# A Mamba layer and a linear attention on one core: the ration of TensorE's work by even and odd slots, and the slot of the convolution's first products

## The chip, the cores and the metric

The kernel runs on one core of one Trainium2 chip. The metric is the device time of one execution in microseconds. Three runs of the kernel before took 8108.69, 8114.99 and 8093.1 us; the median is 8108.69 us.

The engines are named as the profile names them: PE is TensorE (PEld its weight loads), DVE is VectorE, ACT is ScalarE, POOL is GpSimd, SP is SyncE, whose queue issues most DMAs.

## The reference, cut to what matters

The input x is 4 images of 512 channels and 64 x 64 positions. Two layers follow each other, each on a group-normed input and added to it.

```python
x = x + mamba_layer(_gn(x))       # layer 0
x = x + linear_attention(_gn(x))  # layer 1
```

Layer 0 takes the 4096 positions of an image as a sequence, norms each position over its channels, and cuts the channels into 4 groups of 128. Each group is a sequence of its own for the same Mamba block:

```python
xi, z = split(x @ in_proj_w.T)                   # 256 channels each
xc = silu(conv1d(xi, 4 taps) + conv_b)
dt, Bs, Cs = split(xc @ x_proj_w.T)              # rank 8, 16 states, 16 states
dt = softplus(dt @ dt_proj_w.T + dt_proj_b)
h = exp(dt * A) * h + (dt * xc) * Bs             # a scan over the positions, per channel and state
y = (sum over states of h * Cs + xc * D_param) * silu(z)
y = y @ out_proj_w.T
```

A skip is added, the result is normed again over the channels and projected. Layer 1 forms q, k (with relu) and v, sums k times q over all positions of an image, and only then can apply that sum to v and project. So an image's attention begins when its last Mamba tile is through.

## The kernel before, in words

**Steps and slots.** The work is cut into 128 steps: image b, tile t of 512 positions, channel group c (the innermost). A step is done in 16 slots (`SLOTS`), one for each half e of the 256 inner channels, each of four groups q of states and each half jj of the blocks of channels. The loop thus has 2048 slots. Slot s of a step in the text is the slot with that number, 0 to 15.

**What a slot issues** (`slot`, from line 618, and the functions that it calls). On POOL `drive(g + 2)` makes the input bx of the slot two ahead (L614, 128x1024). On DVE there are two scans (L632, 128x512); behind each of them ACT makes the decay dA of a scan three ahead (L606). After the first scan comes `product(g - 1)` (L655): the states of the slot before are multiplied by c_all, which TensorE has spread over the partitions into a PSUM bank of its own (`c_row`, one bank, one c_all for two slots). The exception is in `BEHIND`, the slots 4 and 11: their product comes at the end of the slot itself, so that a wide DVE operation which stands at the end of slot 3 or 10 (`AWAY`) has its place. After the product of an odd slot, TensorE is given the next c_all, and then `fold_states`, which sums the states into y. The last quarter of the positions is multiplied on POOL instead (L643).

So DVE's order around slot 4 is: two scans of slot 3, a wide operation or none, scan, product(3), scan, product(4), two scans of slot 5 and so on. TensorE's c_all for the slots 4 and 5 can only start after product(3), since it overwrites the bank that product(3) reads, and product(4) is the first to need it. The c_all for slots 6 and 7 starts after product(5) and is first needed by product(6), in slot 7.

**What else a slot carries** is issued by `after()`, at the end of each slot, by the slot's number:
- slots 0 and 1: the last parts of `mixers` of the step after the next; the spread of d_all in slot 1
- slot 2: `time_banks`, two banks pt for the step width dt; slot 3: `time_steps`, two softplus on ACT that read them (L512), between two loads of ACT's table
- slots 3, 5, 6, 7, 8 and 9: one part each of `inputs` (`front`) of the step after the next. The first part is two taps of the convolution for one half (pc, two products of 128x512), the second the other two taps; the third and fourth do the same for the other half; the last two are pz
- slot 4: `to_rows`, on POOL (L520) and as DMAs on SP, and `out_proj` (po, three products' worth)
- slot 6: the copy of po back (L690), and, as due one slot after the second part of `inputs`, the copy of pc (L484)
- slots 10 and 12 to 15: silu, and the parts of `mixers`

**Three queues of pieces** fill in the rest: `ahead` (the norm of the next tile), `late` (the norm and projection of the tile just done) and `rest` (the attention of an image that is done, which runs beside the next image's Mamba). Each slot takes at most one piece of each. Whether it may depends on `credit`: each slot adds its ration, takes away the products that were issued since (`work["mm"]`, in which a 128x512 fp32 product counts 1, bf16 a quarter, and four abreast count a quarter each), and what is saved up is limited. A piece of `late` or `rest` is issued while the credit is above zero. The pieces' wide DVE operations (L386, L406) go to slots 3 and 10.

**Banks.** The products of `inputs`, of `time_banks`, `out_proj`, `mixers` and of all pieces share three PSUM banks (`ps_w`), handed out in turn: whoever takes a bank waits until the engine that reads its last content is done. TensorE works in the order of issue, so what is behind a waiting product waits too.

Of the kernel before, what the change touches and what calls it, by code (L numbers as in the profile page):

```python
# [24 lines left out]
def kernel(  # L25
# [100 lines left out]
    work = {"mm": 0.0}  # L126
# [376 lines left out]
    def time_banks(f, nm):  # L503

        f["pt"] = [work_bank(f"pt_{nm}_{e}", 0) for e in range(NH)]
        for e in range(NH):
            r = slice(e * LANE, (e + 1) * LANE)
            mm(f["pt"][e], w_dt[r, :], f["dtr"][r, :], start=True, stop=True, abreast=NH)
# [16 lines left out]
    def spread(f, e, nm):  # L525

        d = wk.tile([P, 2, NJ, T], F32, tag="d_all", name=f"d_all_{nm}_{e}")
        for v in range(2):
            src = f["d_rows", v].rearrange("(j i) e t -> i e j t", i=BLK)[:, e]
            for k in range(KS):  # L530
                nc.sync.dma_start(d[k * BLK : (k + 1) * BLK, v], src)  # L531
        f["d_all", e] = d

    def mixers(f, nm):

        pd = work_bank(f"pd_{nm}", 0)
        for e in range(NH):
            mm(pd, w_xp[:, e, :], f["xz"][:, 0, e, :], start=(e == 0), stop=(e == NH - 1))  # L540
        yield
        f["both"] = wk.tile([P, 2, NH, T], F32, tag="dt", name=f"dt_{nm}", bufs=1)
        dtr = f["dtr"] = f["both"][0 : 2 * LANE, 1, NH - 1, :]
        nc.scalar.copy(dtr, pd[0 : 2 * LANE, :])
        b_rows = f["b_rows"] = dram.tile([NST, T], F32, tag="b_rows", name=f"b_rows_{nm}", bufs=3)
        c_rows = f["c_rows"] = dram.tile(
            [NST, T - CUT], F32, tag="c_rows", name=f"c_rows_{nm}", bufs=3
        )

        def rows_out():  # L550
            nc.sync.dma_start(b_rows, dtr[RANK : RANK + NST, :])
            nc.sync.dma_start(c_rows, dtr[LANE : LANE + NST, CUT:])

        later(1, rows_out)
        parts = f["parts"] = wk.tile([P, CUT], BF16, tag="parts", name=f"parts_{nm}", bufs=3)
        nc.scalar.copy(parts, pd[:, :CUT])
        for i in (2, 3):
            yield
            mm(pd[:, :CUT], minus, parts, start=False, stop=True, skip_group_check=True)
            yield  # L560
            nc.scalar.copy(parts[i * LANE :, :], pd[i * LANE :, :CUT])
# [113 lines left out]
    def take_y(f, n, e):  # L675
        nc.scalar.copy(f["xz"][:, 0, e, :], ys.pop((n, e)))  # L676

    def gate(f, e):
        nc.gpsimd.tensor_tensor(  # L679
            f["xz"][:, 1, e, :], f["xz"][:, 1, e, :], f["xz"][:, 0, e, :], ALU.mult  # L680
        )
# [234 lines left out]
    def input_norm(b):  # L916
        stats = stats_tile(f"st0_{b}")
        yield from stats0(stats, b)
        norms[b] = yield from stats_end(stats, f"a{b}")
        yield  # L920

    def tile_norm(b, t):
        xn[b, t] = wk.tile([P, NC, NTAP - 1 + T], F32, tag="xn", name=f"xn_{b}_{t}", bufs=3)
        pads[b, t] = small.tile([P, NC, NTAP - 1], F32, tag="pad", name=f"pad_{b}_{t}")
        yield from normed(
            xn[b, t], pads[b, t], pads[b, t - 1] if t else None, b, t, norms[b]
        )
# [13 lines left out]
    def step_inputs(n):  # L941
        b, t, c = steps[n]
        return inputs(fs[n], xn[b, t], c, names[n])
# [6 lines left out]
    def add_to(queue, pieces):  # L950
        queue.append([pieces, None])
# [40 lines left out]
    with tc.manual_schedule():  # L992
        credit, seen, mix, held[0], held_x[0] = 0.0, work["mm"], iter(()), 0, 0
        for n, (b, t, c) in enumerate(steps):
            f, nm = fs[n], names[n]
            before = fs[n - 1] if n else None
            nxt = fs[n + 1] if n + 1 < N else None
            front = step_inputs(n + 2) if n + 2 < N else iter(())
            last_mix, mix = mix, mixers(fs[n + 2], names[n + 2]) if n + 2 < N else iter(())
            if c == 0 and (t + 1 < NT or b + 1 < B):  # L1000
                add_to(ahead, tile_norm(b, t + 1) if t + 1 < NT else tile_norm(b + 1, 0))
            if c == 0 and t == 0 and b + 1 < B:
                add_to(light, input_norm(b + 1))
            assert c != 2 or not ahead
            for s in range(SLOTS):
                def after():
                    nonlocal credit, seen
                    now[0] = n * SLOTS + s
                    for what in [w for at, w in due if at <= now[0]]:
                        what()  # L1010
                    due[:] = [d for d in due if d[0] > now[0]]
                    if s == 0 and before is not None:
                        take_y(before, n - 1, 1)
                    if s == SLOTS // 2:
                        take_y(f, n, 0)
                    if s < 2:
                        next(last_mix, None)
                    if s == 1:
                        spread(f, 1, nm)
                        if before is not None:  # L1020
                            gate(before, 1)
                    if s == 2 and nxt is not None:
                        time_banks(nxt, names[n + 1])
                    if s == 3 and nxt is not None:
                        nc.scalar.preload_act_table_set("softplus")
                        time_steps(nxt, names[n + 1])
                        nc.scalar.preload_act_table_set("natural_log_exp_and_others")
                    if s == 6 and before is not None:
                        pb_, pt_, pc_ = steps[n - 1]
                        with_skip(before, xn[pb_, pt_], pc_)  # L1030
                        if pc_ == NC - 1:
                            add_to(late, leave(pb_, pt_))
                    if s in (3, 5, 6, 7, 8, 9):
                        next(front, None)
                    if s == 4 and nxt is not None:
                        to_rows(nxt, 0, names[n + 1])
                        to_rows(nxt, 1, names[n + 1])
                    if s == 4 and before is not None:
                        pb_, pt_, pc_ = steps[n - 1]
                        out_proj(before, xn[pb_, pt_], pc_, names[n - 1])  # L1040
                    if s == 9:
                        gate(f, 0)
                        if nxt is not None:
                            spread(nxt, 0, names[n + 1])
                    if s == 10 and n + 2 < N:
                        silu(n + 2)
                        nc.scalar.preload_act_table_set("natural_log_exp_and_others")
                    if s >= 12:
                        next(mix, None)
                    may = [  # L1050
                        what for k, what in ((0, "wide"), (1, "one ahead"), (2, "two ahead"))
                        if any(a - 2 * k <= s <= a - k for a in AWAY) or (k == 2 and s == SLOTS - 1)
                    ]
                    if light and light[0][1] == "wait" or s in AWAY and not any(
                        q and q[0][1] == "wide" for q in (ahead, late)
                    ):
                        one(light)

                    limit[0] = 1 if 0 < s < 6 else 2
                    credit = min(credit + 3.5 - (work["mm"] - seen), 2.6)  # L1060
                    busy = False
                    for queue in (ahead, late, rest):
                        kind = queue[0][1] if queue else None
                        if queue is ahead or kind == "free" or credit > 0 or kind == "more" and not busy:
                            start = work["mm"]
                            one(queue, ANYWHERE if queue is ahead and (c, s) > (1, 4) else may)
                            credit -= work["mm"] - start
                            busy = busy or work["mm"] - start > 1
                    seen = work["mm"]

                slot(n * SLOTS + s, N * SLOTS, after)
            fs[n - 1].clear() if n else None
        product(N * SLOTS - 1, N * SLOTS)
        now[0] = None
        for _, what in due:
            what()
# [60 lines left out]
```

## Time and profile before

| | before |
|---|---|
| median of 3 runs | 8108.69 us |
| profiled execution: time | 8103.21 us |
| profiled execution: span | 8101.5 us |
| loop, first scan to last product | 118.7 to 7631.7 us |
| DVE busy | 7158.1 us (88% of the span) |
| POOL busy | 6888.6 us (85%) |
| PE busy | 6487.2 us (80%) |
| ACT busy | 5365.5 us (66%) |
| mean granted clock of PE | 0.887 |

A group line of the profile reads: line, engine, operation, tiles written and read (buffer numbers left out), shapes, count | busy us, mean ns of one | idle time of the engine just before them, and what ended most of it. In a timeline, the first number is the start in us from the start of the span, the second the time taken, and brackets hold the idle time before it with what ended it. The granted clock is the share of TensorE's full speed that its throttle let through.

### The profile page before, as it was taken

The page shows a single profiled execution, that of the slowest core. Times are in us where ns is not written, and L with a number is a line of the kernel's source. Part 1 is how long each engine was busy: PE and PEld are TensorE (multiplying, and loading weights), DVE is VectorE, ACT ScalarE, POOL GpSimd, SP SyncE. Part 2 cuts the span into 40 slices and gives each one's busy share as a digit, 9 for nine tenths or more (in the row PEclk, how much of TensorE's full clock was granted, in tenths as well). Part 3 has the DMA queues.
Part 4 walks back from the last instruction along what each step waited for, and adds up shares of the span by engine and source line. Part 5 has one row for each costly group of instructions (what it writes and reads, how often), then busy time and mean ns, then how long its engine had stood idle before and what let it go on. Part 6 is the DMA issues. An engine that isn't in the chain of part 4 may idle for free.

```text
span 8101.5 us, 92105 instructions
## 1 busy us (share of the span) xinstructions
PE 6487.2 (80%) x24800; PEld 2116.5 (26%) x24800; DVE 7158.1 (88%) x6891; ACT 5365.5 (66%) x7841; POOL 6888.6 (85%) x4597
## 2 busy tenths in 40 slices
PE   5677777667888888887788888888788888888699
PEld 1111112111222222322132222222122222322144
DVE  5999999999999999999999999999999999999700
ACT  4666677676677767676777767676777777766421
POOL 4999999999999988899989989898999989889600
PEclk8787878788899999998898999899799999999699
DMA  5666666666666666676756666677666666677402
GB/s 159 167 164 159 154 147 153 157 155 166 162 169 156 156 161 153 173 191 169 170 144 171 165 163 159 149 182 184 157 163 157 154 154 148 157 185 187 113 32 88
DMA packets 829195, 1265.95 MB, mean 156 GB/s; under 512 B 183912, under 2 KB 317560, under 8 KB 816384
## 3 DMA queue, kind: packets, MB, share of 16 engines
q1 hardware_dynamic: 804736, 1222.32, 60.1%
q0 software_dynamic: 16896, 33.56, 2.4%
q10 hardware_dynamic: 7040, 4.20, 0.2%
q8 instruction: 194, 3.18, 0.2%
q14 instruction: 329, 2.70, 0.1%
HBM read 1052.78 MB, written 206.57 MB: 155 GB/s over the span
## 4 chain that ended last, share of the span: by engine, by line
DVE 21%; PE 19%; DMA 19%; POOL 15%; issue 10%; SPq 9%; ACT 6%; POOLq 0%; DVEq 0%; ACTq 0%
DVE h L632 13%; POOL bx L614 11%; DMA d_all<-d_rows 11%; DVE h L655 6%; SPq L581 6%; PE pq L124 5%; DMA b_all<-b_rows 4%; SPq L531 3%; ACT dA L606 3%; PE pc L124 3%; PE pr L124 3%; PE y L124 2%; DMA c_sb<-c_rows 2%; POOL h L643 2%; POOL dt L520 1%
## 5 line engine op out<-in xcount | busy, mean ns | idle before, releaser
L614 POOL TENSOR_TENSOR bx<-d_all,b_all 128x1024 f32<-128x1024 f32 x2048 | 4815.8, 2370 | 51.4 <-DVE h L632 34.1
L632 DVE TENSOR_TENSOR_SCAN h<-dA,st,bx 128x512 f32<-128x512 f32 x3584 | 4425.2, 1268 | 59.0 <-ACT dA L606 49.5
L606 ACT ACTIVATE dA<-d_all,a_t 128x512 f32<-128x512 f32 x4096 | 2787.8, 689 | 1936.0 <-DVE h L632 1893.6
L655 DVE TENSOR_TENSOR h<-h,c_all 128x768 f32<-128x768 f32 x2048 | 1908.8, 932 | 301.9 <-PE c_all L124 293.5
L643 POOL TENSOR_TENSOR h<-h,c_sb 128x512 f32<-128x512 f32 x1024 | 1298.6, 1268 | 145.8 <-DMA c_sb<-c_rows 49.7
L124 PE MATMUL y<-h,fold 128*32 128x512 f32 x8192 | 1287.8, 705 | 140.7 <-POOL h L643 136.9
L124 PE MATMUL c_all<-parts,sel 128*128 128x384 bf16 x1024 | 369.8, 361 | 1112.7 <-DVE h L655 1110.5
L124 PE MATMUL pc<-xn,w_cv 128*128 128x512 f32 x2048 | 1068.2, 657 | 189.4 <-DVE xn L406 127.2
L124 PE MATMUL pq<-w_qk,xa 128*128 128x512 f32 x2048 | 989.8, 616 | 1.6 <-ACT xa L344 1.6
L632 DVE TENSOR_TENSOR_SCAN h<-dA,bx 128x512 f32<-128x512 f32 x512 | 601.6, 1207 | 60.3 <-ACT dA L606 55.9
L124 PEld LDWEIGHTS pc<-xn,w_cv 128*128 128x128 f32 x2048 | 394.1, 203 | 819.3 <-issue 455.9
L124 PEld LDWEIGHTS <-sel 128*128 128x128 bf16 x1280 | 127.5, 100 | 1792.5 <-DVE h L655 1552.8
L642 POOL COPY st<-h 128x4 f32<-128x4 f32 x1024 | 207.3, 202 | 436.4 <-DVE h L632 392.9
L124 PEld LDWEIGHTS pq<-w_qk,xa 128*128 128x128 f32 x2048 | 404.2, 200 | 455.6 <-issue 432.3
L124 PE MATMUL pr<-xb,m 128*128 128x512 f32 x1024 | 503.8, 630 | 7.3 <-DMA xb<-x 4.0
L124 PE MATMUL pp<-xn,w_pr 128*128 128x512 f32 x1024 | 487.5, 602 | 3.8 <-DVE xn L406 3.8
L124 PEld LDWEIGHTS y<-h,fold 128*32 128x32 f32 x8192 | 171.0, 115 | 719.2 <-issue 291.0
L124 PE MATMUL y<-xz,dg 32*32 32x512 f32 x2048 | 340.5, 741 | 0.0
L679 POOL TENSOR_TENSOR xz<-xz 128x512 f32<-128x512 f32 x256 | 325.0, 1270 | 2.7 <-ACT xz L676 2.7
L124 PE MATMUL pd<-xz,w_xp 128*128 128x512 f32 x512 | 317.3, 752 | 7.8 <-ACT xz L946 7.8
L520 POOL TENSOR_TENSOR dt<-dt,xz 128x1024 f32<-128x1024 f32 x128 | 302.1, 2360 | 22.1 <-DMA c_rows<-dt 20.9
L730 ACT ACTIVATE kq<-pq 128x512 f32<-128x512 f32 x256 | 150.9, 590 | 242.9 <-PE pq L124 240.0
(156 smaller groups left out, 5919.5 us busy)
## 6 DMA issues: line engine op xcount, KB each, us to landing
d_all<-d_rows SPq DMA_DIRECT2D x2048, 256.0 KB, 6.6
b_all<-b_rows SPq DMA_DIRECT2D x4096, 64.0 KB, 2.2
d_rows<-dt SPq DMA_DIRECT2D x256, 512.0 KB, 3.7
c_sb<-c_rows SPq DMA_DIRECT2D x4096, 16.0 KB, 1.8
xs<-in_x_dram SPq DMA_DIRECT2D x32, 1024.0 KB, 6.5
xn<-in_x_dram SPq DMA_DIRECT2D x32, 1024.0 KB, 5.8
xr<-in_x_dram POOLq DMA_DIRECT2D x32, 1024.0 KB, 10.6
x<-xr SPq DMA_DIRECT2D x32, 1024.0 KB, 6.6
```

The costliest lines, as they stand in the source:

```text
L124: nc.tensor.matmul(out_, lhsT, rhs, **how)
L520: nc.gpsimd.tensor_tensor(f["both"][:, 1], f["both"][:, 0], f["xz"][:, 0], ALU.mult)
L531: nc.sync.dma_start(d[k * BLK : (k + 1) * BLK, v], src)
L581: nc.sync.dma_start(dst[k * BLK : (k + 1) * BLK, :], rows_[q * KS + k, :].partition_broadcast(BLK))
L606: nc.scalar.activation(dAs[k], fs[n]["d_all", e][:, 0, j, :], AF.Exp, scale=a_t[:, e, j, q : q + 1])
L614: nc.gpsimd.tensor_tensor(bxs[g], fs[n]["d_all", e][:, 1, jj * 2 : jj * 2 + 2, :], bc(b_all[g // JJ], 2), ALU.mult)
L632: nc.vector.tensor_tensor_scan(h[:, j, :], dAs.pop(2 * g + i), bxs[g][:, i, :], 0.0 if t == 0 else st[:, c, e, q, j : j + 1], ALU.mult, AL ...
L642: nc.gpsimd.tensor_copy(st[:, c, e, q, :], h[:, :, T - 1])
L643: nc.gpsimd.tensor_tensor(h[:, :, CUT:], h[:, :, CUT:], bc(c_sb.pop(g // JJ), NJ), ALU.mult)
L655: nc.vector.tensor_tensor(own, own, bc(c_all[g // JJ], 2), ALU.mult)
L679: nc.gpsimd.tensor_tensor(f["xz"][:, 1, e, :], f["xz"][:, 1, e, :], f["xz"][:, 0, e, :], ALU.mult)
L730: nc.scalar.activation(qk[i], pq, AF.Relu)
```

## The change

The first part of `inputs`, the two taps that open the convolution's first bank, is issued in slot 4 instead of slot 3. In slot 4 it stands ahead of `out_proj`, as the code has it.

The ration, 3.5 in every slot with at most 2.6 saved up, becomes 4.5 in even slots with at most 3.4, and 2.5 in odd slots with at most 1.7. Two slots together still get 7. The code that takes pieces by that credit is unchanged.

```diff
@@ -1030,7 +1030,7 @@
                         with_skip(before, xn[pb_, pt_], pc_)
                         if pc_ == NC - 1:
                             add_to(late, leave(pb_, pt_))
-                    if s in (3, 5, 6, 7, 8, 9):
+                    if s in (4, 5, 6, 7, 8, 9):
                         next(front, None)
                     if s == 4 and nxt is not None:
                         to_rows(nxt, 0, names[n + 1])
@@ -1057,7 +1057,9 @@
                         one(light)
 
                     limit[0] = 1 if 0 < s < 6 else 2
-                    credit = min(credit + 3.5 - (work["mm"] - seen), 2.6)
+
+                    credit += (2.5 if s % 2 else 4.5) - (work["mm"] - seen)
+                    credit = min(credit, 1.7 if s % 2 else 3.4)
                     busy = False
                     for queue in (ahead, late, rest):
                         kind = queue[0][1] if queue else None
```

## The prediction

> **What bounds the kernel now.** I read the busy shares first, then the costliest groups with what ended their idle time, then the waits, and last the timeline around the waits that matter. The page of the kernel before:
>
> ```profile
> span 8101.5 us, 92105 instructions
> ...
> PE 6487.2 (80%) x24800; PEld 2116.5 (26%) x24800; DVE 7158.1 (88%) x6891; ACT 5365.5 (66%) x7841; POOL 6888.6 (85%) x4597
> ...
> L632 DVE TENSOR_TENSOR_SCAN h<-dA,st,bx 128x512 f32<-128x512 f32 x3584 | 4425.2, 1268 | 59.0 <-ACT dA L606 49.5
> L655 DVE TENSOR_TENSOR h<-h,c_all 128x768 f32<-128x768 f32 x2048 | 1908.8, 932 | 301.9 <-PE c_all L124 293.5
> ```
>
> The scans start at 118.7 us and the last product ends at 7631.7; what follows (470 us, the last attention) is the same work in both kernels. In the 7514 us between, VectorE is busy 7093.5 us by the window sums, so it sets the time, and its largest wait is the one for c_all: 293.5 us in 172 waits. The most that removing them can bring is those 293.5 us.
>
> I put every such wait into its slot (slot s of a step of 16). Slot 4 has 203.8 us in 95 waits, slot 7 has 54.4 in 38, slot 15 has 30.4 in 31; slots 9 and 11 share the last 4.9. Slot 4 is special: it is in BEHIND, so product(4) follows product(3) after a single scan (about 1.2 us) instead of two, and the c_all that it reads is issued on TensorE only after product(3). The timeline of step 52 shows the form of it (start us, us, engine, instruction, idle time before):
>
> ```profile
> 3129.38 0.93 DVE L655 TENSOR_TENSOR h<-h,c_all 128x768 f32<-128x768 f32 x1
> ...
> 3131.06 1.98 PE L124 MATMUL pc<-xn,w_cv 128*128 128x512 f32 x4 [1.71 <-ACT dt L512]
> ...
> 3132.89 1.88 PE L124 MATMUL pq<-w_qk,xa 128*128 128x512 f32 x4
> ...
> 3134.60 0.33 PE L124 MATMUL c_all<-parts,sel 128*128 128x384 bf16 x1
> ...
> 3134.97 0.95 DVE L655 TENSOR_TENSOR h<-h,c_all 128x768 f32<-128x768 f32 x1 [3.47 <-PE c_all L124]
> ```
>
> product(3) is done at 3130.3. TensorE stands in front of the convolution's first products (pc), whose bank ScalarE still reads, then does those and two attention products, and only then c_all: VectorE loses 3.47 us. Asked for the tile pc, the trace lists 311.3 us of idle TensorE until DVE xn L406 and 116.3 until ACT dt L512: pc in slot 3 often gets a bank whose reader is not done.
>
> A second reading matters as much: the granted TensorE clock. Its records are 1.0 or 0.5, in stretches of 3.41 us. A timeline of a slow stretch, behind 5.09 us of idleness:
>
> ```profile
> 2025.69 0.50 PE L124 MATMUL c_all<-parts,sel 128*128 128x384 bf16 x1 [5.09 <-DVE h L655]
> ...
> 2026.44 1.93 PE L124 MATMUL y<-h,fold 128*32 128x512 f32 x8 [0.24 <-POOL h L643]
> ```
>
> Elsewhere these take 0.34 and 1.06. Over all c_all: with under 2 us of idleness before it, 26 of 781 were slow; with over 2.5 us, 143 of 186. After such a gap in slots 2 and 12 the next 7 us held 4.7 and 5.0 us at half clock, so about 2.35 us of TensorE's time are lost. In slot 4 only 5 gaps exceed 2.5 us, because pc fills slot 3.
>
> **What the Trainium skill says.** "TensorE: Matmul & The Clock Gate", section "What's actually happening", says that the default is the throttled clock and that idleness of about 3.4 us brings it back to half; the records agree (stretches of 3.41 us at 0.5). "Perfetto Trace Analysis", section "Matmuls", says that groups of products should rotate through PSUM banks so that one's evacuation overlaps the next; with three banks here pc waits for an evacuation, as shown. "FP8 and Floating Point Precision", section "TensorE Precision Notes", says that true fp32 takes four passes; with 512 columns and the 2.4 GHz of the first page this is an estimated 0.85 us, and in unbroken stretches the trace has 0.86 us a product (weight loads every 0.43 us, two to a product).
>
> **The change part by part.** Both kernels issue the same 5668 products' worth; what moves is where. From the two schedules, mean products per step (128x512 fp32 counts 1; c_all and fold, 1.19, are in the even slots):
>
> - slots 2+3: 6.8 before, 4.7 after; slot 3 alone 3.0 and 1.0
> - slots 4+5: 7.9 before, 9.2 after; with no ration piece 6.2 and 8.2
> - slots 6+7: 6.1 both, but 28 steps with 8.4 or more after, 3 before
> - slots 12+13: 4.5 before, 5.0 after
>
> Taken away at slot 4: after the change at most 2.2 products stand between product(2) and c_all in slot 3, and where VectorE has a wide operation there (2.27 us, about every second step) they are done during it. In seven steps an attention product takes the bank that the softplus reads, about 1 us each. I leave 10 us of 203.8: **-194 us**. The move of pc issues no DMA; what slot 4 issues on SP (d_rows) and POOL (L520) stays. In slot 4 the first products are queued ahead of out_proj and behind the fold; the copies waiting for both stand in slot 6, and ScalarE has 4.4 us of lead there on average (dA ready before its scan), so they stay hidden; without cover a product is 0.86 us.
>
> Given back in slot 7 (product(6)): its c_all needs TensorE done with slots 4 and 5. Time needed is 0.86 W + 0.47 us (W products in the two slots; before, W = 10.2 gave c_all 3.51 us after product(5), W = 8.2 gave 1.79). From product(3) to product(5) VectorE takes 4 scans and two products, 6.5 us, and 2.0 us more are free until product(6) asks. With c_all prompt at slot 4, lateness is 0.86 W - 5.99; before, three such steps with W = 10.2 had 2.88 to 2.93, the formula 2.78. After, the steps are 59 with W = 8.2, 25 with 9.2, 23 with 10.2, 5 with 11.2 and 13 with 12.2, so waits of 0, 0, 0.78, 1.64 and 2.50 us on the full clock. That alone would be 23 x 0.78 + 5 x 1.64 + 13 x 2.50 = 59 us, no more than the 54.4 there now.
>
> But slot 3 is now thin. VectorE gives the pair of slots 2 and 3 about 6.5 us (8.8 with a wide operation); 40 steps have 3.2 products there (3.2 us), 35 have 4.2 (4.1 us) and 19 have 5.2. Idle time before c_all is then 2 to 5 us. Counting step by step, with the slow starts of slot 2 (53 now), about 62 steps pass 2.5 us: 36 of those with W = 8.2, 13 with 10.2, 13 with 12.2. The nearest row of before agrees: slot 12, behind a load of 3, has 31 of 43 gaps over 2.5 us. Each adds 2.35 us: 36 x 1.4 + 13 x 3.1 + 13 x 4.85 + 10 x 0.78 + 5 x 1.64 = 50 + 40 + 63 + 8 + 8 = 169 us. Against 54.4: **+115 us**. Bounds: 59 us (no slow clock) and about 250 (94 steps slow).
>
> Slot 9 (product(8)): 28 steps with 8.4 to 9.4 products in slots 6+7 are 1.0 us late with a prompt c_all(6) and 1.9 with a late one; 28 x 1.5 = 42 against 4.2: **+38 us**. Slot 15: by the before rows of equal load (slots 12+13 with 4+2 products: 0.25 us each, with 5+2: 1.56) 47 us, by the smaller bursts in slot 13 no change; I take 34: **+3 us**.
>
> The small waits of VectorE for pk, pob and pm (about 25 us now) move to slots 4 to 9, where TensorE is late: +5. POOL, busy 6877 us in the loop, had 5 us idle per step; if VectorE ran ahead by all of slot 4's wait, its bx lead would run out and give back 19 to 29 us; with most returned at slot 7 I take +6. Sum: -194 + 115 + 38 + 3 + 5 + 6 = **-27 us**. The profiled execution took 8103.2 us (span 8101.5), the median of the runs is 8108.7; I set the sum against the latter: **8082 us**.
>
> **The rivals.**
> - *The clock stays full.* If products left in slot 3 and work still running in slot 2 keep TensorE awake, slot 7 costs 59, slot 9 about 24; the sum is -194 + 5 + 20 + 3 + 5, and POOL and ScalarE take 30 back: -131, 7978 us. For it: the clock records are of one execution; against: 143 of 186 long gaps were slow.
> - *Slower: the slow clock is the rule at slot 4.* If all 94 steps with at most 5.2 products in slots 2+3 start at half clock, 32 more pay 2.3 us, 74 us: +47, 8156 us. It decides from about 75 steps on, where the 27 us are gone. For it: the slow state outlasts moderately busy stretches in the records.
> - *POOL is the real limit.* Its ops need about 54.7 us of a step's 58.7; then what VectorE gains appears as waits for bx: about 8105 us. Against: VectorE waits only 12.1 us for bx now.
> - *The ration does nothing:* excluded, since 54 rows fewer of TensorE's order and the loads above show the shift.
>
> **How the numbers follow.** A change under 0.3% (24 us) can't be told from none here. The likeliest case, the wait moved from slot 4 to slots 7 and 9, gets 0.50, with its own range 8050 to 8120; full clock 0.27; slow clock as the rule 0.18; POOL 0.05. Faster by over 0.3%: all of the full-clock case and half of the likeliest, 0.51. Within: 0.24 of the likeliest, 0.05 of POOL, 0.02 of the slow case, 0.31. Slower: 0.18. The range, 7970 to 8150, takes in the full-clock case and most of the slow one.
>
> **What would show it.** Right: waits for c_all in slot 4 near 10 us, in slot 7 above 130 and in slot 9 above 25; over 50 gaps above 2.5 us before c_all in slot 4, and half clock there; the sum of c_all waits near 260. Idle time until DVE xn L406 before pc gone. Wrong: slot 7 near 60 us (the clock held), or waits for bx or dA above 60 us (another engine took over), or a tail not near 470 us.

## The result and the profile after

The changed kernel takes 8202.42 us in the median of four runs (8185.39 to 8210.91), the kernel before beside it 8104.42 (8093.1 to 8114.99): a ratio of 1.0121, 95% interval 1.0108 to 1.0134. It is slower, and above the range that was predicted. The profiled execution took 8185.39 us, 82 more than that of before; the median grew by 98. The page after:

```profile
span 8183.3 us, 92137 instructions
...
PE 6553.7 (80%) x24800; PEld 2129.7 (26%) x24800; DVE 7170.4 (88%) x6891; ACT 5359.6 (65%) x7841; POOL 6887.2 (84%) x4597
...
L632 DVE TENSOR_TENSOR_SCAN h<-dA,st,bx 128x512 f32<-128x512 f32 x3584 | 4425.8, 1267 | 120.2 <-ACT dA L606 97.6
L655 DVE TENSOR_TENSOR h<-h,c_all 128x768 f32<-128x768 f32 x2048 | 1907.4, 931 | 307.0 <-PE c_all L124 291.8
...
L124 PE MATMUL pc<-xn,w_cv 128*128 128x512 f32 x2048 | 1056.0, 648 | 13.7 <-ACT xz L484 8.7
```

Three things stand out. TensorE hardly waits in front of pc any more: the idleness of these products is 13.7 us now, and on the page of before their line was

```profile
L124 PE MATMUL pc<-xn,w_cv 128*128 128x512 f32 x2048 | 1068.2, 657 | 189.4 <-DVE xn L406 127.2
```

VectorE's waits for c_all add up to the same as before, 291.8 us for 293.5. And its waits for dA in the scans grew: in this group the idleness until dA went from 49.5 to 97.6 us.

The loop runs from 118.6 to 7713.5 us, 82 us longer than before; what follows it took 470 us in both. So all of it lies in the loop. VectorE's waits there, put into their slots (us, and times):

| VectorE waits for | before | after |
|---|---|---|
| c_all, slot 4 | 203.8 (95) | 40.4 (29) |
| c_all, slot 7 | 54.4 (38) | 172.7 (82) |
| c_all, slot 9 | 4.2 (6) | 41.1 (26) |
| c_all, slot 15 | 30.4 (31) | 35.5 (21) |
| dA, slot 5 | 8.4 (5) | 41.8 (25) |
| dA, slot 12 | 48.4 (45) | 63.5 (47) |
| dA, all (46 of it ahead of the first scan) | 105.4 | 156.9 |
| all waits, with these 46 | 465.7 | 535.3 |

The waits grew by 70 us; the other 12 us are what is left of the loop's time without them, VectorE's own work.

What slot 7 looks like now is seen in the timeline of step 98 of the kernel after (start, us, engine, instruction, idle time before it):

```profile
5937.00 0.50 PE L124 MATMUL c_all<-parts,sel 128*128 128x384 bf16 x1 [3.63 <-DVE h L655]
...
5937.43 1.94 PE L124 MATMUL y<-h,fold 128*32 128x512 f32 x8
...
5939.30 3.25 PE L124 MATMUL pc<-xn,w_cv 128*128 128x512 f32 x4
...
5947.01 1.88 PE L124 MATMUL pc<-xn,w_cv 128*128 128x512 f32 x4
...
5948.73 1.88 PE L124 MATMUL pp<-xn,w_pr 128*128 128x512 f32 x4
...
5950.44 0.33 PE L124 MATMUL c_all<-parts,sel 128*128 128x384 bf16 x1
...
5950.81 0.95 DVE L655 TENSOR_TENSOR h<-h,c_all 128x768 f32<-128x768 f32 x1 [5.21 <-PE c_all L124]
```

TensorE stood idle for 3.63 us in slot 3 and starts c_all for slot 4 at half clock: c_all 0.50 us where 0.33 is full speed, the fold 1.94 for 1.06, the first two products of pc 3.25 for 1.88. With 12.2 products in slots 4 and 5 it gets to the next c_all at 5950.44, and product(6) has waited 5.21 us.

ScalarE's part is seen in step 60 of the kernel after, across slots 3 to 5:

```profile
3669.49 1.28 ACT L1025 ACT_TABLE_LOAD   x1
...
3670.79 1.27 ACT L512 ACTIVATE dt<-pt,dtb 128x512 f32<-128x512 f32 x2
...
3672.08 1.28 ACT L1027 ACT_TABLE_LOAD   x1
...
3673.37 1.52 ACT L344 ACTIVATE xn<-xn,off_a,gr_a 128x512 f32<-128x512 f32 x2
...
3674.80 1.28 ACT L606 ACTIVATE dA<-d_all,a_t 128x512 f32<-128x512 f32 x2
...
3675.50 2.46 DVE L632 TENSOR_TENSOR_SCAN h<-dA,st,bx 128x512 f32<-128x512 f32 x2 [1.28 <-ACT dA L606]
```

From 3669.49 to 3674.80 ScalarE makes no decay: a table load, two softplus, a table load and two parts of the norm stand in its order. Slot 4 no longer has VectorE waiting over that block, so the scan in slot 5 waits for dA. (The price of a load agrees with the Trainium skill, "ScalarE activation tables: per-element evaluation and per-set limits", section "What a function is on this engine": 1283 ns.)

### The profile page after: what moved, and what is told of

It reads as the page before. It is cut to its first block, busy times and chain, and to the rows that moved or that the text cites. A ratio compares the mean times of both kernels' runs of the same rounds, so it can differ in the third digit from the quotient of the medians.

```text
span 8183.3 us, 92137 instructions
## 1 busy us (share of the span) xinstructions
PE 6553.7 (80%) x24800; PEld 2129.7 (26%) x24800; DVE 7170.4 (88%) x6891; ACT 5359.6 (65%) x7841; POOL 6887.2 (84%) x4597
## 4 chain that ended last, share of the span: by engine, by line
DVE 24%; PE 21%; DMA 15%; POOL 12%; issue 11%; ACT 8%; SPq 7%; POOLq 0%; DVEq 0%; ACTq 0%
DVE h L632 15%; POOL bx L614 9%; DMA d_all<-d_rows 9%; DVE h L655 8%; PE pq L124 5%; SPq L581 4%; PE pc L124 4%; DMA b_all<-b_rows 3%; ACT dA L606 3%; PE y L124 3%; SPq L531 2%; PE pr L124 2%; PE po L124 2%; POOL h L643 2%; DMA c_sb<-c_rows 1%
## 5 line engine op out<-in xcount | busy, mean ns | idle before, releaser
L632 DVE TENSOR_TENSOR_SCAN h<-dA,st,bx 128x512 f32<-128x512 f32 x3584 | 4425.8, 1267 | 120.2 <-ACT dA L606 97.6
L655 DVE TENSOR_TENSOR h<-h,c_all 128x768 f32<-128x768 f32 x2048 | 1907.4, 931 | 307.0 <-PE c_all L124 291.8
L124 PE MATMUL y<-h,fold 128*32 128x512 f32 x8192 | 1343.6, 734 | 135.1 <-POOL h L643 129.5
L124 PE MATMUL pc<-xn,w_cv 128*128 128x512 f32 x2048 | 1056.0, 648 | 13.7 <-ACT xz L484 8.7
L124 PE MATMUL pp<-xn,w_pr 128*128 128x512 f32 x1024 | 510.8, 631 | 3.8 <-DVE xn L406 3.8
```

The lines of the kernel that those rows point to most:

```text
L124: nc.tensor.matmul(out_, lhsT, rhs, **how)
L632: nc.vector.tensor_tensor_scan(h[:, j, :], dAs.pop(2 * g + i), bxs[g][:, i, :], 0.0 if t == 0 else st[:, c, e, q, j : j + 1], ALU.mult, AL ...
L655: nc.vector.tensor_tensor(own, own, bc(c_all[g // JJ], 2), ALU.mult)
```

## The experiments

The tables of slots in this part are my counts from the traces, as above. "Half clock behind slot 4" is the sum, over the 128 steps, of the time at half clock in the 7 us after c_all for slot 4 starts: 38 us before, 320 us after.

### One part of the change alone

`e1_move` moves the first products and keeps the old ration:

```diff
-                    if s in (3, 5, 6, 7, 8, 9):
+                    if s in (4, 5, 6, 7, 8, 9):
```

> The move alone, with the old ration of 3.5. Theory 1 (the move carries the loss: VectorE's wait goes from slot 4 to slot 7 with TensorE on half clock, and ScalarE's softplus with its two table loads is uncovered in slot 5): c_all waits about 35 us in slot 4, 170 to 190 in slot 7, 10 in slot 9; waits for dA in slot 5 about 40 us; 8120 to 8200 us. Theory 2 (the ration carries the loss): the move alone gains, 7980 to 8070 us, with slot 7 below 100 us.

Measured: 8159.69 us (8143.39 to 8173.78), ratio 1.0079 (1.006 to 1.0098). The first theory holds, with more of the wait in slot 7 (197.3 us) and less of dA in slot 5 (28.6) than it said.

`e2_ration` changes the ration and keeps the first products in slot 3:

```diff
-                    credit = min(credit + 3.5 - (work["mm"] - seen), 2.6)
+                    credit += (2.5 if s % 2 else 4.5) - (work["mm"] - seen)
+                    credit = min(credit, 1.7 if s % 2 else 3.4)
```

> The ration alone, with the first products left in slot 3. Theory 1: smaller pieces in slot 3 shorten slot 4's waits from 204 to about 150 us, slots 7 and 9 gain 10 to 20, dA in slot 5 stays below 15: 8030 to 8090 us, not slower than before. Theory 2: 8170 to 8220 us.

Measured: 8144.98 us (8134.27 to 8147.58), ratio 1.0059 (1.0044 to 1.0074). Both theories missed: the time lies between the two ranges.

Each edit alone makes the kernel slower, and 0.79% and 0.59% come near the 1.21% of both. Neither is the guilty one and neither is harmless. By slots they do different things:

| waits, us | before | move | ration | both |
|---|---|---|---|---|
| c_all, slot 4 | 203.8 | 46.4 | 185.3 | 40.4 |
| c_all, slot 7 | 54.4 | 197.3 | 49.8 | 172.7 |
| c_all, slot 9 | 4.2 | 18.2 | 23.1 | 41.1 |
| dA, slot 5 | 8.4 | 28.6 | 23.5 | 41.8 |
| DMA of xr, slot 5 | 0 | 0 | 30.7 | 4.4 |
| half clock behind slot 4 | 38 | 324 | 32 | 320 |

The move is what empties slot 4, fills slot 7 and lets TensorE's clock fall. The ration takes only 18 us off slot 4, and pays in small waits. One of them shows in the timeline of step 63 under the ration alone:

```profile
3805.73 1.29 POOL L461 DMA_DIRECT2D xr<-in_x_dram  x1
...
3820.41 1.29 DVE L464 BATCH_NORM_STATS2 st<-xr 128x6 f32<-128x512 f32 x2 [3.45 <-DMA xr<-in_x_dram]
```

The residual's read is issued by POOL in slot 2, the statistics that need it come in slot 5, and the read took 14.7 us to land. Under the ration alone nine reads were issued in slot 2; they took 13.8 to 16.0 us to land, and the statistics came some 11 us after the issue. Those issued in slot 0 landed after 10.2 to 12.5 us, and no statistics waited for them. So the shifted ration puts the piece into a slot from which its read comes too late; why a read takes longer from there was not looked into.

### The clock: fill the idle time

`e3_warm` is the changed kernel with products of zeros in slot 3, added to the open y bank. They add nothing to the result, and bring slots 2 and 3 up to 5.3 or 7.3 products (`mark` is the count of products at the end of slot 1):

```diff
+                    if s == 3:
+                        for k in range(int((5.3 if c % 2 else 7.3) - (seen - mark))):
+                            nc.tensor.matmul(
+                                ys[n, 0], zero.to_broadcast([P, P]),
+                                w_cv[:, 0:2, :].rearrange("p k d -> p (k d)"),
+                                start=False, stop=False, skip_group_check=True,
+                            )
```

> The changed kernel with TensorE kept busy at the end of slot 3: up to four extra products with a column of zeros for weights, added into the open y bank, which change nothing in it; they fill slots 2 and 3 up to 5 products in odd steps and 7 in even ones. Theory 1: c_all(4) then starts on full clock; half clock after it falls from 320 us in all to below 120, slot 7 from 173 to 60 to 100 us, the kernel gains 60 to 110 us on the changed one: 8090 to 8140 us. If half clock is not the cause of slot 7's wait: slot 7 stays above 150 us and the time within 20 us of 8202, or longer.

Measured: 8196.68 us (8190.68 to 8205.27), ratio 1.0123 (1.0106 to 1.014): no gain, where 8090 to 8140 us were expected. Its page:

```profile
L657 DVE TENSOR_TENSOR h<-h,c_all 128x768 f32<-128x768 f32 x2048 | 1910.8, 933 | 355.6 <-PE c_all L124 346.5
```

The clock was cured: half clock behind slot 4 fell from 320 to 62 us. Slot 7's wait fell by 48 us, from 172.7 to 124.6. But the filler stood in front of c_all, and slot 4's wait rose from 40.4 to 147.6 us. The run gives the clock's price, though not a better kernel. Split by the products in slots 4 and 5, slot 7's wait in the changed kernel, and with the filler, is (steps x mean us):

| products | after, half clock | after, full clock | filler, full clock |
|---|---|---|---|
| 8.2 | 36 x 0.87 | 23 x 0.01 | 44 x 0.13 |
| 9.2 | 10 x 2.14 | 15 x 0.03 | 25 x 0.58 |
| 10.2 | 3 x 3.13 | 20 x 1.77 | 21 x 1.56 |
| 11.2 | 1 x 3.58 | 4 x 2.60 | 5 x 2.74 |
| 12.2 | 13 x 4.64 | none | 13 x 3.22 |

Row by row against steps of the same load at full clock (for 12.2, those with the filler), half clock makes some 75 us of slot 7's 173; the filler took 48 off, with 17 steps still slow. So the clock is between a quarter and somewhat under half of this wait, and the larger part is the amount of work.

### ScalarE's block: shorten it in both kernels

`e4_exp_after` is the changed kernel with exp in place of softplus and without the two table loads around it. It leaves out the logarithm of the step width, so the decays have other values; the number and size of all other instructions stay.

```diff
-                f["both"][:, 0, e, :], f["pt"][e], AF.Softplus, bias=dtb[:, e : e + 1]
+                f["both"][:, 0, e, :], f["pt"][e], AF.Exp, bias=dtb[:, e : e + 1]
...
-                        nc.scalar.preload_act_table_set("softplus")
                         time_steps(nxt, names[n + 1])
-                        nc.scalar.preload_act_table_set("natural_log_exp_and_others")
```

> The changed kernel with the softplus of the step width replaced by an exponential of the table that is loaded anyway, so that the two table loads in slot 3 fall away (2.56 us of ScalarE per step); the step width is computed differently, all else stays. Theory 1: waits for dA in slot 5 fall from 42 us to below 10 and the time falls by 20 to 60 us, to 8140 to 8180; part returns as waits for c_all in slot 7. If ScalarE's block did not matter: within 15 us of 8202.

Measured: 8153.39 us (8138.81 to 8154.6), ratio to the kernel before 1.0068 (1.0053 to 1.0083). The wait for dA in slot 5 is gone (41.8 to 0), and slot 4's for c_all fell from 40.4 to 16.8. It looked as if the block, uncovered, was the loss. That needs the same edit in the kernel before:

> The kernel before, with softplus replaced by exp (so time steps and outputs change) and without the two table loads around it in slot 3: the control for the same edit in the changed kernel, which brought 49 us (8202 to 8153). Theory A (ScalarE's block in slot 3 costs only where the wait of slot 4 no longer covers it): it brings 15 us or less here, 8085 to 8110, with the wait for dA in slot 5 falling from 8 us to about 0; so with the block gone the change still costs about 50 us, not 98. Rival (the block costs both kernels alike): about 49 us here too, 8055.

Measured: 8017.64 us (8015.41 to 8020.25), ratio 0.989 (0.9873 to 0.9906). Theory A falls, and its rival too: the edit brings the kernel before 1.1%, more than the changed one (1.0121 to 1.0068, about 0.5%). There it shows in another place:

```profile
L655 DVE TENSOR_TENSOR h<-h,c_all 128x768 f32<-128x768 f32 x2048 | 1906.8, 931 | 222.4 <-PE c_all L124 210.9
```

c_all in slot 4 fell from 203.8 to 115.1 us. So the edit pays in both kernels, before the change at the banks that TensorE waits for and after it mostly at dA. That it is the block's length which counts in the kernel before is not shown; the next experiment looks at which bank TensorE waits for. Without the block the change costs more, not less: 1.0068 over 0.989 is 1.8%.

### The softplus one slot earlier

The next edit leaves nothing out. The two table loads and the softplus go from slot 3 to slot 2, right behind their products:

```diff
-                    if s == 3 and nxt is not None:
+                    if s == 2 and nxt is not None:
                         nc.scalar.preload_act_table_set("softplus")
                         time_steps(nxt, names[n + 1])
```

In the changed kernel:

> The changed kernel with its two table loads and softplus one slot earlier, in slot 2 behind their products; nothing is left out. Theory A: the wait for dA in slot 5 falls from 42 us to under 15, and slot 4's wait for c_all from 40 us to about 20, because the softplus's banks come free a slot earlier; 8150 to 8170. Rival (the block's length counts, not its place): the wait moves to dA of slot 4 or to slot 3, and the time stays at 8190 to 8210.

Measured: 8157.19 us (8152.26 to 8166.51), ratio 1.0064 (1.0049 to 1.0079). The time is as Theory A has it, the way is half the rival's: dA in slot 5 fell to 0 and c_all in slot 4 to 6.3, but 81.2 us of waits for dA came up in slot 4.

In the kernel before:

> The kernel before with the same earlier softplus. Theory A: little is there to be had in dA (8 us), but slot 3's first products of the convolution wait for the softplus's bank (116 us of idle TensorE), so slot 4's wait for c_all falls from 204 us to about 150; 8060 to 8085. Rival: the block now delays dA of slot 4, 8105 or more.

Measured: 8012.02 us (8005.34 to 8017.51), ratio 0.9884 (0.9869 to 0.9898). This one line beats both kernels. Its page:

```profile
L632 DVE TENSOR_TENSOR_SCAN h<-dA,st,bx 128x512 f32<-128x512 f32 x3584 | 4423.8, 1267 | 111.2 <-ACT dA L606 94.3
L655 DVE TENSOR_TENSOR h<-h,c_all 128x768 f32<-128x768 f32 x2048 | 1906.6, 931 | 144.6 <-PE c_all L124 130.8
```

The waits for c_all were more than halved, 293.5 to 130.8: 203.8 to 57.4 in slot 4 and 54.4 to 29.0 in slot 7, against 66.1 us of new waits for dA in slot 4. Those new waits stand ahead of product(4) and cover some of c_all's; c_all and dA of slot 4 together fell from 204 to 124 us. With exp, where no such cover arises, 115 were left. So either edit takes 80 to 90 us off slot 4, where I had expected about 50.

The way was not the expected one. Asked for the tile pc, the trace has no less idle time until ACT dt L512 than before (133.3 us in 122 waits, 116.3 in 56 before); what fell is the idle time until DVE xn L406, from 311.3 us in 122 waits to 61.0 in 26. (These counts take the products and their weight loads apart, so the 122 waits are 61 steps and the 26 are 13; the products alone waited 127.2 us before, as their line above says.) By what TensorE last waited for ahead of c_all for slot 4, VectorE's wait there divides so (us, and steps):

| TensorE waited last for | before | exp | softplus in slot 2 |
|---|---|---|---|
| DVE xn L406, with pc | 90.4 (51) | 17.9 (10) | 13.0 (6) |
| ACT dt L512, with pc | 70.3 (27) | 60.4 (38) | 22.4 (10) |
| ACT res L877, with pc | 18.5 (7) | 15.9 (7) | 0 |
| others | 24.5 (10) | 20.9 (9) | 22.0 (27) |

All three kernels issue the same products in the same order. So most of the gain is that pc gets another bank, seldom the one that the wide operation L406 still reads; "in turn", as said of the banks above, is too simple. The softplus's own bank coming free earlier is the smaller part (70.3 to 22.4 us), and with exp there is hardly any of it. Why the bank that pc gets changes with the softplus, no run shows, and a run that changes the bank alone was not made. Step 46 shows the other bank. The kernel before:

```profile
2767.32 2.26 DVE L406 TENSOR_TENSOR xn<-xn,var_b 128x2048 f32<-128x2048 f32 x1
...
2769.43 1.26 ACT L512 ACTIVATE dt<-pt,dtb 128x512 f32<-128x512 f32 x2
...
2769.63 2.43 PE L124 MATMUL pc<-xn,w_cv 128*128 128x512 f32 x4 [2.93 <-DVE xn L406]
...
2770.69 0.93 DVE L655 TENSOR_TENSOR h<-h,c_all 128x768 f32<-128x768 f32 x1
...
2772.28 2.96 PE L124 MATMUL pq<-w_qk,xa 128*128 128x512 f32 x4
...
2775.08 0.33 PE L124 MATMUL c_all<-parts,sel 128*128 128x384 bf16 x1
...
2775.44 0.95 DVE L655 TENSOR_TENSOR h<-h,c_all 128x768 f32<-128x768 f32 x1 [2.63 <-PE c_all L124]
```

With the softplus in slot 2:

```profile
2756.32 1.27 ACT L512 ACTIVATE dt<-pt,dtb 128x512 f32<-128x512 f32 x2
...
2756.79 2.26 DVE L406 TENSOR_TENSOR xn<-xn,var_b 128x2048 f32<-128x2048 f32 x1
...
2757.06 1.98 PE L124 MATMUL pc<-xn,w_cv 128*128 128x512 f32 x4 [0.88 <-ACT dt L512]
...
2759.09 1.88 PE L124 MATMUL pq<-w_qk,xa 128*128 128x512 f32 x4
...
2760.17 0.93 DVE L655 TENSOR_TENSOR h<-h,c_all 128x768 f32<-128x768 f32 x1
...
2761.15 0.34 PE L124 MATMUL c_all<-parts,sel 128*128 128x384 bf16 x1 [0.17 <-DVE h L655]
...
2762.39 0.95 DVE L655 TENSOR_TENSOR h<-h,c_all 128x768 f32<-128x768 f32 x1
```

Before, pc waits 2.93 us, until the wide operation L406 ends (2767.32 + 2.26) and lets its bank go. The attention's products pq stand behind it, c_all behind them, and product(4) waits 2.63 us. With the softplus earlier, pc waits for the first half of the softplus instead, starts while L406 still runs, and is through with pq when product(3) ends; c_all starts right behind it. The wait for the bank came with a fall of the clock: pq takes 2.96 us for 1.88, and in the 61 steps whose pc waited for L406 the records of pc took 3.05 us in the mean, where 1.98 is full speed.

### The two edits again, on the kernel with the earlier softplus

If the move were harmless but for ScalarE's block in slot 3, it would cost nothing here. First the move, as in `e1_move`:

> The kernel before with the softplus in slot 2 (8012 us), and of the change the moved first products alone. Theory C (slot 4's wait was one for the softplus's banks; the move removes it only by carrying two products into slots 4 and 5 behind an idle, half-clocked slot 3): slot 4's wait for c_all falls from 57 us to under 15, slot 7's rises from 29 us to about 160, half clock behind slot 4 from 36 us to over 300, dA of slot 4 rises to about 80; 8095 to 8130. Rival (the move costs only by uncovering ScalarE's block in slot 3, which is gone here): 8000 to 8040.

Measured: 8114.47 us (8104.87 to 8119.92), ratio to the kernel before 1.0007 (0.9998 to 1.0016), so 1.2% above its own base. Slot 4's wait for c_all fell from 57.4 to 1.0 us, slot 7's rose from 29.0 to 154.9, half clock behind slot 4 from 36 to 347, dA in slot 4 from 66.1 to 78.4. Theory C holds in each of its numbers, though in the kernel before slot 4's wait was more often one for L406's bank than for the softplus's. Then the ration, as in `e2_ration`:

> The kernel before with the softplus in slot 2, and of the change the ration alone. Theory C: it adds about what it adds to the kernel before (0.6%, 48 us), in small waits: the residual tile's DMA in slot 5, c_all in slot 9, dA; 8045 to 8070. Rival (its cost comes of ScalarE's block too): 8000 to 8025.

Measured: 8050.8 us (8031.96 to 8058.92), ratio 0.9927 (0.9911 to 0.9943), 0.4% above its base. The wait for xr in slot 5 is again there (36.6 us in nine waits), and c_all in slot 9 (29.0 us, from 5.0). As ratios to the kernel before:

| softplus in | neither edit | move | ration | both |
|---|---|---|---|---|
| slot 3 | 1 | 1.0079 | 1.0059 | 1.0121 |
| slot 2 | 0.9884 | 1.0007 | 0.9927 | 1.0064 |

In both rows the edits about add up. Against their own row's first entry, the move and both together cost more in the second row (1.2% and 1.8%), the ration less (0.4%).

### The amount of work in slots 4 and 5

`e8_split` keeps the move and the old ration, and spreads the parts of `inputs` otherwise: the second products in slot 6 in place of slot 5, and both pz in slot 9.

```diff
-                    if s in (4, 5, 6, 7, 8, 9):
+                    if s in (4, 6, 7, 8, 9):
                         next(front, None)
+                    if s == 9:
+                        next(front, None)
```

> The moved first products with the old ration, and the convolution's second products not in slot 5 but in slot 6, the rest in 7 and 8 and both gate products in slot 9; nothing is left out. Mean products in slots 4+5 fall from 9.5 to 7.7, no step has over 9.2 (65 of 128 had 10.2 or more), 6+7 rise from 6.0 to 6.8. Theory B (slot 7's wait comes of the amount of work in slots 4 and 5, the half clock adds some 1.4 us to half of the steps): slot 7's wait falls from 197 us to about 70, slot 9's rises from 18 to about 50, slot 4 stays near 45; 8060 to 8080, faster than the kernel before. Rival (the half clock behind slot 4 alone makes slot 7's wait): slot 7 stays above 140 us, about 8130 to 8150. Rival (POOL or ScalarE take back what VectorE gains): waits for dA or bx rise by over 60 us, 8110 or more.

Measured: 8124.1 us (8117.33 to 8129.01), ratio 1.0023 (1.0014 to 1.0032). It is faster than the move alone (1.0079), but missed the expected 8060 to 8080. The time is that of the second rival, whose sign came only in part: waits for dA rose by 36 us, with the 46 ahead of the first scan left out, and those for bx did not. Slot 7's wait halved, 197.3 to 95.8 us, of which 63.7 lie in the 75 steps with over 2 us of half clock behind slot 4: the amount of work counts, and so does the clock. Slot 9 rose to 49.3, as expected. Not expected was dA in slot 12, from 54.9 to 96.6 us:

```profile
L632 DVE TENSOR_TENSOR_SCAN h<-dA,st,bx 128x512 f32<-128x512 f32 x3584 | 4427.1, 1267 | 116.0 <-ACT dA L606 108.3
L655 DVE TENSOR_TENSOR h<-h,c_all 128x768 f32<-128x768 f32 x2048 | 1908.4, 932 | 246.2 <-PE c_all L124 231.6
```

The same spreading on the kernel with the earlier softplus, the first products left in slot 3 (`if s in (3, 6, 7, 8, 9)`):

> The kernel before with the softplus in slot 2, first products still in slot 3, the second ones in slot 6, the rest in 7 and 8, and both gate products in slot 9; nothing is left out. Products in slots 4+5 fall from 7.9 to 6.3 a step, those in 6+7 rise from 6.1 to 7.1, with 37 steps of 9 or more. Theory C: slot 7's wait falls from 29 us to under 8, slot 9's rises from 5 us to about 45, and dA of slot 12, behind later copies, from 49 us to 70 or more; 8030 to 8060, no gain. Rival (any product taken out of slots 4 and 5 is won): 7970 to 7990.

Measured: 8112.28 us (8096.48 to 8118.94), ratio 1.0004 (0.9995 to 1.0012), so 1.2% slower than without it and worse than both expectations. The signs were right: slot 7 fell from 29.0 to 9.8 us, slot 9 rose from 5.0 to 40.4, dA in slot 12 from 48.6 to 88.6; dA in slot 4 (66.1 to 81.3) and the small waits for pk (3.1 to 14.8) I had not counted. In both kernels with two pz in slot 9, dA in slot 12 rose by about 40 us; that the copies of pz hold up the silu on ScalarE is likely, but was not tried alone.

## Why the prediction was wrong

The sum of the prediction, term by term, against the two profiled executions:

| term | predicted, us | measured, us |
|---|---|---|
| c_all, slot 4 | -194 | -163 |
| c_all, slot 7 | +115 | +118 |
| c_all, slot 9 | +38 | +37 |
| c_all, slot 15 | +3 | +5 |
| pk, pob, pm and the like | +5 | +2 |
| POOL (bx) | +6 | +9 |
| ScalarE (dA) | 0 | +52 |
| DMA of xr, waits too short to have a releaser, other c_all | 0 | +10 |
| VectorE's own time in the loop | 0 | +12 |
| sum (of terms not rounded) | -27 | +82 |

**What was right.** The work moves from slot 4 to slots 7 and 9, and TensorE falls to half clock behind slot 4. The loads are exact (59, 25, 23, 5 and 13 steps). The predicted 62 steps that pass into half clock were 65 (steps with over 2 of the 7 us at half clock), the 36 with 8.2 products and the 13 with 12.2 exactly. That TensorE would no longer wait for xn L406 in front of pc was right too.

**What was luck.** That slot 7 came out at +118 for +115 is in part luck, because errors cancel. The 36 slow steps with 8.2 products cost 0.87 us each for 1.4. Ten slow steps with 9.2 cost 2.14 each, where nothing was put. With 10.2 only three were slow for 13, but at full clock the price was 1.77 for 0.78. Of the predicted 169 us the clock was to make 110; it made some 48 to 75 of 173. Nor were the slow steps those that the forecast looked for: it expected over 50 gaps above 2.5 us ahead of c_all in slot 4, the trace has 21, and 34 of the 65 slow steps have under 1.5 us there. Counted anywhere between the c_all for slot 2 and that for slot 4, TensorE was idle 2.8 us in the mean in the slow steps and 1.4 us in the others.

**The rivals.** The rival "the clock stays full" fell (320 us of half clock behind slot 4 for 38), and so did "the slow clock is the rule": it has 94 slow steps and is decided from 75 on. "POOL is the real limit" fell with 21 us of waits for bx (its need of 54.7 us a step was a slip: 6877 us over 128 steps are 53.7).

**The step that failed first** is "ScalarE has 4.4 us of lead there on average (dA ready before its scan), so they stay hidden". I had taken the lead from the wrong slot: 4.4 us is the mean of slot 4's two scans (4.04 and 4.72 us), and slot 6's are 3.64 and 2.39. At the second scan of slot 5, the first decay behind the softplus, it was 2.94 us in the mean, 1.80 in the first step of each tile and 0.03 at the least. In the kernel after the mean is 1.89, and the wait in slot 5 rose from 8 to 42 us. The wait in slot 4 was the cover of that block: the step asked what hides the moved work, but not what the removed wait had been hiding. The run with exp shows it in the changed kernel: without the block the wait in slot 5 is gone, and the time falls by 49 us. The forecast's own sign that another engine took over, waits for dA above 60 us, came: without the 46 ahead of the first scan they are 111 us, 59 before. The remainder of their growth lies mostly in slot 12 (+15), which I traced no further.

**The second** is the size of what is left in slot 4: 40 us for 10. I counted seven steps in which a piece takes the bank that the softplus reads, at 1 us each; 29 steps waited. Seven of them did stand behind the softplus's bank, but cost 15.1 us. In twelve, 11.3 us, a piece waited for L406's bank, which the forecast had left out, and the other ten make 14 us.

**What the forecast never asked** is why pc was late in slot 3. The prediction quotes the wait for the bank, and then takes the products themselves as what has to go. Moving the softplus shows that slot 4 loses 80 us of waits, c_all and dA taken together, with pc still in slot 3, when pc gets another bank or its bank comes free earlier; and slot 7's wait falls by 25 us with it. The move takes 157 us (203.8 to 46.4) and gives 143 back in slot 7, because two more products stand in slots 4 and 5, behind a slot 3 too thin to keep the clock up. So the move had next to nothing to win, and ScalarE and the ration's small waits made it a loss. The sign hung on terms of 10 to 50 us that I had set to nothing.

**Open** is how the ration alone comes to its 0.4 to 0.6%: the waits that I can name (xr 31 us, slot 9 19, dA in slot 5 15, less 18 in slot 4) come to 47, near the 45 us by which its loop is longer, beside smaller ones of both signs (slot 15 13 us less, VectorE's own time 8 more). Which piece causes which was only followed for xr. Open is also why pc gets another bank when the softplus moves.

## What to carry to other kernels

Before moving work out of the way of a wait, ask what the first instruction in that queue waits for: here a bank, and one line that changed which bank it was and when it came free brought 1.2%, where moving the work lost 0.8%. A wait that is removed was also a cover; read the lead of every other engine at the slots just behind it, with its minimum and not only its mean. And work taken out of one stretch of an in-order engine lands in the next one, and may leave the first so thin that the clock falls as well.

## What the runs showed of the hardware that I had not expected

The granted clock of TensorE has a memory. Cut into stretches of 3.41 us, in the trace of the kernel before, full clock was kept after 96 of 101 stretches that were about 60% busy, after 71 of 111 at 50% and 3 of 48 at 40%. From half clock it came back after 0 of 46 stretches at 70%, 5 of 64 at 80%, 28 of 32 at 90% and 209 of 232 at 100%. The Trainium skill, "TensorE: Matmul & The Clock Gate", section "What's actually happening", speaks of an idle window that loses the full clock and a busy one that regains it. In this trace the window need not be idle: stretches half busy lost the full clock in 40 of 111 cases and those at 40% in 45 of 48, while at half clock only 5 of 110 stretches 70 or 80% busy regained it, and 237 of 264 at 90% or more. So one thin slot can cost slots 4 and 5 up to 6.8 us at half clock, the most that a step of the kernel after has.
